# Attention with 49 of 64 block products: the row sums move from VectorE to accumulating transfers issued by GpSimd, and the scores are computed four slots earlier

## The chip, the cores and the metric

The kernel runs on one core of a Trainium2 chip. The core has TensorE (PE; its weight loads are listed as PEld), VectorE (DVE), ScalarE (ACT), GpSimd (POOL) and SyncE (SP), each with its own in-order queue, and 16 DMA engines that the queues share. SyncE issues nearly all transfers of this kernel. The metric is the device time of one execution in microseconds. Before the change the median of three runs is 3673.21 us (3672.21 to 3676.82).

## The reference, cut to what matters

Two layers are applied to x of shape (2, 512, 64, 64) in float32. The first is a deformable convolution, which the change does not touch. The second is attention over the 4096 pixels of each image:

```python
px = transpose(group_norm(x))                  # (2, 4096, 512)
q, k, v = tanh(px @ Wq.T), tanh(px @ Wk.T), px @ Wv.T
attn = softmax(einsum('bip,bjp,p->bij', q, k, align_w), axis=2)
content = (px + attn @ v) @ Wfc.T + bfc
x = x + relu(batch_norm(content))
```

So every query needs 4096 exponentials of scores, their sum (the softmax's denominator) and their product with the values. The residual px enters the same product.

## The kernel before, in words

All of the attention is in the part of the kernel that begins at L1242. The values are multiplied by Wfc ahead of time, so that one product gives the content.

**Chunks, blocks and slots.** An image is worked on in four chunks of 1024 queries, so there are eight chunks in all. The queries of a chunk are in two halves (`qh`), the keys in groups `g` of 512 (NG = 8 groups), and each group in two halves. A score tile `e0`, `e1`, `e2` or `e3` of one group holds the exponentials of one half of the keys against one half of the queries: `e0` and `e2` belong to the first query half, `e1` and `e3` to the second. Each tile has 128 partitions of 1024 numbers, 512 KB. The product with the values is a two-level scheme that needs seven products where a plain one has eight, used twice over: 7 x 7 = 49 block products in place of 64. It needs sums and differences of blocks, and these are VectorE's work. A chunk takes 7 products `p` of 9 steps each (eight groups, and a ninth for the residual), so 63 slots (SLOTS); `ORDER` (L1378) says which tile each product uses. In a slot TensorE does seven block matmuls (L1478), each recorded twice, with weights `v` that SyncE loads three slots ahead (`fetch`, L1570; four buffers).

**The order of the work.** It is written out by hand. `Attention.slot` (L1592) issues the work of one slot in program order, and each engine keeps to it. `EVENTS` (L1541) says in which slot a score tile is made; negative slots belong to the end of the chunk before, which overlaps with the start of the next one from slot 44 on. `produce` (L1389) makes a tile: two score matmuls into the one PSUM buffer `pS` and an exponential on ScalarE. `settle` (L1417) follows one slot later on VectorE. It adds a first-half tile to the running total, and replaces the second block of each tile by the difference of its two blocks (`transform`, L1385). For `e1` it also calls `second_row` (L1410), which turns `e0` into `e1 - e0` and `e1` into `e1 + e3` and adds the latter to the second half's total. `inner_sums` (L1454) makes `tt`, three more block sums, for the slot LEAD = 4 ahead; there are five buffers of `tt`.

**The row sums.** `add_total` (L1403) keeps one total per query half, `tot`. The first tile is copied, and each later one is added by VectorE. `total` (L1426) adds the two blocks of 512 numbers of the total on VectorE, in slots 4 and 21. One slot later `spread_total` (L1432) multiplies by a matrix of ones on TensorE, so that the sum over the partitions stands in all of them. TensorE waits there for `total`, and what follows on TensorE waits behind it. `scale_residual` (L1446) then multiplies the residual by the sum, and in slots 7 and 25 the reciprocal is taken. The sum for the ninth step of a product cannot be made before that. For this reason `sums` for slots 8 and 26 comes late, in slots 6 and 24.

**Buffers and start.** Score tiles, totals, residuals and products `ct` share one ring of 36 pieces (`w1ring`, L1245). At the start of each image the values are computed first (`values`, L1622). The tiles with negative slots of its first chunk are made between them (`early_scores`, L1674), and those left over in one go at the end. In that stretch GpSimd has some additions of its own (`sum_pixels`, L1303).

Of the kernel before, what the change touches and what calls it, by code (L numbers as in the profile page):

```python
# [10 lines left out]
F32 = mybir.dt.float32  # L11
I32 = mybir.dt.int32
AF = mybir.ActivationFunctionType
ALU = mybir.AluOpType
# [4 lines left out]
P = 128  # L19
# [508 lines left out]
NG = S // P // 4  # L528
# [6 lines left out]
def kernel(ctx: ExitStack, tc: tile.TileContext, t_in: dict, out: bass.AP):  # L535
# [7 lines left out]
    nc.vector.tensor_reduce(al[:, 1:2], al[:, 0:1], AX.X, ALU.max, apply_absolute_value=True)  # L543
    nc.vector.memset(al[:, 0:1], 1.0 / SCORE_MAX)
    window_path(tc, t_in, out, far, sums)


# [27 lines left out]
def window_path(ctx: ExitStack, tc: tile.TileContext, t_in: dict, out: bass.AP, far: bass.AP, sums: bass.AP):  # L575
    nc = tc.nc
# [66 lines left out]
    with ExitStack() as l0:  # L643
# [517 lines left out]
        with tc.manual_schedule():  # L1161
# [60 lines left out]
            for i in range(NSEQ):  # L1222
# [6 lines left out]
                w, m, g = Chain(weights, i + 1), Chain(sample, i), Chain(features, i + 3)  # L1229
# [12 lines left out]
    with ExitStack() as l1, tc.manual_schedule():  # L1242
        HC = C // 2
        HQ = CH // 2
        ring = l1.enter_context(tc.tile_pool(name="w1ring", bufs=36, reuse_waits="tile"))  # L1245
        bnp = l1.enter_context(tc.tile_pool(name="w1bnp", bufs=1))
        bst = bnp.tile([P, KB, NB * NCH, 6], F32, name="bst")
        bfc = load("L1_conv_bfc", [P, KB], None, bnp)
# [3 lines left out]
        def piece(name, shape=(P, 2, CH)):  # L1252
            return ring.tile(list(shape), F32, tag="r", name=name)
# [15 lines left out]
        with ExitStack() as inner:  # L1269
            wk = inner.enter_context(tc.tile_pool(name="w1work", bufs=1))  # L1270
# [94 lines left out]
            def load_queries(n, k):  # L1365
                q = wk.tile([P, 2, CH], F32, name="q")
                for h in range(2):
                    nc.sync.dma_start(q[h * DQ : (h + 1) * DQ], q_d[n][k])
                return q
# [12 lines left out]
            def blocks(t):  # L1382
                return t.rearrange("p a (s q) -> p (a s) q", s=2)

            def transform(t):  # L1385
                x = blocks(t)
                nc.vector.tensor_sub(x[:, 1], x[:, 1], x[:, 0])
# [14 lines left out]

            def add_total(c, qh, t):  # L1403
                if qh in c.tot:
                    nc.vector.tensor_add(c.tot[qh], c.tot[qh], t)  # L1405
                else:
                    c.tot[qh] = piece("tot")
                    nc.vector.tensor_copy(c.tot[qh], t)

            def second_row(c, g):  # L1410
                t0, t1 = c.e["e0", g], c.e["e1", g]
                nc.vector.tensor_sub(t0, t1, t0)  # L1412
                nc.vector.tensor_add(t1, t1, c.e["e3", g])  # L1413
                if g < NG:
                    add_total(c, 1, t1)

            def settle(c, key, g):  # L1417

                e = c.e[key, g]
                if key in ("e0", "e2"):  # L1420
                    add_total(c, 0, e)
                transform(e)
                if key == "e1":
                    second_row(c, g)

            def total(c, qh):  # L1426
                t = c.tot[qh]
                nc.vector.tensor_add(t[:, 1, :], t[:, 1, :], t[:, 0, :])
                if qh:
                    nc.vector.tensor_add(t[:, 1, HQ:], t[:, 1, HQ:], t[:, 0, :HQ])  # L1430

            def spread_total(c, qh):  # L1432
                p = pair_bank("pr")[:, 0, :]
                nc.tensor.matmul(p, ones, c.tot.pop(qh)[:, 1, :], start=True, stop=True)
                nc.scalar.copy(rin[:, qh, :], p)

            def load_residual(c, qh):
                x = load_chunk(c.n, 2 * c.k + qh, nc.sync, "xq")
                for h in range(2):
                    c.e[f"e{2 * h + qh}", NG] = x[h]  # L1440

            def norm_residual(c, qh):
                for h in range(2):
                    normalize(c.e[f"e{2 * h + qh}", NG], 2 * h, *norms[c.n])

            def scale_residual(c, qh):  # L1446
                for h in range(2):
                    t = c.e[f"e{2 * h + qh}", NG]
                    nc.vector.tensor_mul(t, t, rin[:, qh, :].unsqueeze(1).to_broadcast([P, 2, CH]))
                    transform(t)  # L1450
                if qh:
                    second_row(c, NG)
# [14 lines left out]
            def products(c, p, g, v, t):  # L1467
                if g == 0:
                    c.acc = bank("accx"), bank("accy")
                ax, ay = c.acc  # L1470
                x = blocks(c.e[ORDER[p][0], g])
                for out, blk, op, first, final in (
                    (ax[:, 0], 0, x[:, 0], True, False), (ax[:, 1], 2, x[:, 2], False, True),
                    (ax[:, 2], 4, t[:, 0], True, True),
                    (ay[:, 0], 3, t[:, 2], True, False), (ay[:, 1], 1, x[:, 1], False, True),
                    (ay[:, 2], 5, x[:, 3], True, False), (ay[:, 3], 6, t[:, 1], False, True),
                ):
                    nc.tensor.matmul(out, v[:, blk, :], op, start=(first and g == 0), stop=(final and g == NG))  # L1478

            def first_copy(c):  # L1480
                ax, ay = c.acc
                u = wk.tile([P, HQ], F32, name="u", bufs=2)
                nc.scalar.copy(u, ax[:, 0])  # L1483
                return u

# [53 lines left out]
                    yield from finish(c, t, 1, 0)  # L1539

            EVENTS = {}  # L1541
            for g, l in enumerate((-14, -13, -11, -10, -9, -7, -6, -5)):
                EVENTS.setdefault(l, []).append(("e0", g))
            for g in range(NG):
                EVENTS.setdefault(g - 4, []).append(("e2", g))
                EVENTS.setdefault(5 + g, []).append(("e3", g))
                EVENTS.setdefault(13 + g, []).append(("e1", g))

            class Attention:

# [5 lines left out]
                def before(self, l, c):  # L1556

                    for done in self.open:
                        settle(*done)
                    self.open = []  # L1560
                    for key, g in EVENTS.get(l, ()):
                        produce(c, key, g)
                        self.open.append((c, key, g))
# [10 lines left out]
                def at(self, l, c, s):  # L1574

                    if l in (-7, 8):
                        load_residual(c, int(l > 0))
                    if l in (-3, 11):
                        norm_residual(c, int(l > 0))
                    if l in (5, 22):  # L1580
                        spread_total(c, int(l > 5))
                        scale_residual(c, int(l > 5))
                    if l in (7, 25):
                        nc.vector.reciprocal(rin[:, int(l > 7), :], rin[:, int(l > 7), :])
                    if l in (6, 24):
                        self.sums(s + 2)
                    if 30 <= l < 31 + NG:
                        nc.vector.tensor_add(c.e["e3", l - 30], c.e["e0", l - 30], c.e["e3", l - 30])
                    if 40 <= l < 41 + NG:
                        nc.vector.tensor_sub(c.e["e2", l - 40], c.e["e2", l - 40], c.e["e3", l - 40])  # L1590

                def slot(self, s):  # L1592
                    k, l = divmod(s, SLOTS)
                    c = self.chunks[k]
                    nxt = self.chunks[k + 1] if k + 1 < NCH // 2 else None
                    self.fetch(s + 3)
                    if l % (NG + 1) == 0 and self.ends:
                        next(self.ends[-1], None)
                    self.before(l, c)
                    if nxt and l >= 44:  # L1600
                        if l == 44:
                            nxt.q = load_queries(self.n, k + 1)
                        self.before(l - SLOTS, nxt)
                        self.at(l - SLOTS, nxt, s)
                    self.at(l, c, s)
                    if l + LEAD not in (8, 26):
                        self.sums(s + LEAD)
                    if l in (4, 21):
                        total(c, int(l > 4))
                    p, g = divmod(l, NG + 1)  # L1610
                    products(c, p, g, self.v.pop(s), self.t.pop(s))
                    for e in self.ends[:-1] if g == 0 else self.ends:
                        next(e, None)
                    if g == NG:
                        self.ends = self.ends[-1:] + [collect(c, p, first_copy(c), c.acc)]
# [50 lines left out]
            for n in range(NB):  # L1666
# [1 line left out]
                first = at.chunks[0]  # L1668
                pending = []
                early_events = deque(  # L1670
                    (l, key, g) for l in range(-16, 0) for key, g in EVENTS.get(l, ())
                )

                def early_scores():  # L1674
# [76 lines left out]
                for done in at.open:  # L1751
                    settle(*done)
# [5 lines left out]
                for s in range(NCH // 2 * SLOTS):  # L1758
                    at.slot(s)
                    l = s - (NCH // 2 - 1) * SLOTS  # L1760
# [88 lines left out]
```

## Time and profile before

| | |
|---|---|
| median of three runs | 3673.21 us |
| the profiled execution | 3674.86 us |
| its span | 3673.1 us |
| busy: PE, PEld, DVE, ACT, POOL | 3239.0, 2261.1, 2969.6, 1362.9, 272.5 us |
| mean granted TensorE clock | 0.949 |
| DMA | 537.67 MB, 146 GB/s over the span |
| additions to `tot` at L1405 | 176, 1221 ns each, 214.9 us |
| exponentials at L1400 | 256, 1023 ns each |

Busy time counts an engine's instructions, and a wait shows as idle time before an instruction, with the instruction or transfer that released it. The attention lies between about 1300 and 3590 us of the span. The spreads of the second query half, which mark the chunks, start at 1543.5, 1791.1, 2039.4 and 2286.5 us for the first image and at 2701.1, 2948.4, 3196.7 and 3445.4 us for the second.

### The profile page before, as it was taken

To read this page: it belongs to the slowest core of one execution; us is meant where nothing else is said; L and a number is where in the kernel's file an instruction comes from. 1 tells how busy PE (TensorE), PEld (TensorE's weight loads), DVE (VectorE), ACT (ScalarE), POOL (GpSimd) and SP (SyncE) were. 2 spreads that over 40 slices of the span, in tenths; PEclk is the share of its full clock that TensorE was granted. 3 is DMA by queue.
4 is the path that set the end of the run, shared out by engine and by line. 5 is a ranking of instruction groups with operands and counts; after the bars stand their busy time and mean duration, and the time that the engine had idled before them with its cause. 6 is when DMAs were issued, how large, how long until landed. Compare 5 with 4: busy or idle time off the path is not lost.

```text
span 3673.1 us, 37956 instructions
## 1 busy us (share of the span) xinstructions
PE 3239.0 (88%) x14147; PEld 2261.1 (62%) x14147; DVE 2969.6 (81%) x4107; ACT 1362.9 (37%) x1802; POOL 272.5 (7%) x186
## 2 busy tenths in 40 slices
PE   5789999999998867899899898998889989899890
PEld 2355555555555645686676776876577676686670
DVE  8899999999995577877887878778787787877864
ACT  2577778778775312203112022022202202203105
POOL 1121121121120110000000000011000000000000
PEclk9889999999999978999999999999899999999995
DMA  6334334334232454344353443555434344344379
GB/s 211 97 116 139 120 100 127 109 108 131 94 105 102 163 198 160 117 147 151 116 160 123 135 151 108 185 175 202 156 121 154 123 142 139 113 151 146 113 299 349
DMA packets 201634, 537.67 MB, mean 146 GB/s; under 512 B 25024, under 2 KB 26816, under 8 KB 200416
## 3 DMA queue, kind: packets, MB, share of 16 engines
q1 hardware_dynamic: 193920, 514.18, 41.9%
q10 hardware_dynamic: 7488, 20.97, 1.7%
q8 instruction: 113, 1.85, 0.2%
q14 instruction: 81, 0.66, 0.1%
q0 software_dynamic: 32, 0.00, 0.0%
HBM read 410.15 MB, written 124.91 MB: 146 GB/s over the span
## 4 chain that ended last, share of the span: by engine, by line
PE 63%; DVE 27%; DMA 4%; ACT 3%; issue 1%; POOL 1%; SPq 0%; ACTq 0%; DVEq 0%; POOLq 0%
PE accy L1478 20%; PE accx L1478 16%; DVE conv L820 9%; PE py L1004 6%; PE pS L1396 5%; PE pq L789 5%; PE pa L984 5%; DVE tot L1405 2%; DVE e L1412 2%; DVE e L1413 2%; PE pvy L1633 2%; PE pk L1700 1%; DVE tt L1458 1%; DVE vform L1332 1%; PE pvx L1633 1%
## 5 line engine op out<-in xcount | busy, mean ns | idle before, releaser
L1478 PE MATMUL accy<-tt,v 128*128 128x256 f32 x2016 | 602.2, 380 | 0.0
L1400 ACT ACTIVATE e<-pS 128x1024 f32<-128x1024 f32 x256 | 261.8, 1023 | 895.0 <-PE pS L1396 785.6
L1478 PE MATMUL accx<-e,v 128*128 128x256 f32 x1792 | 489.1, 396 | 25.8 <-DMA v<-wv 15.3
L1478 PEld LDWEIGHTS accx<-e,v 128*128 128x128 f32 x1792 | 329.5, 193 | 226.4 <-issue 153.1
L1478 PE MATMUL accy<-e,v 128*128 128x256 f32 x1792 | 461.7, 380 | 0.0
L820 DVE SCALAR_TENSOR_TENSOR conv<-xn,L_conv_dw_w_sb,conv 128x504 f32<-128x504 f32 (+1 forms) x512 | 409.4, 808 | 36.6 <-ACT conv L814 22.7
L1478 PEld LDWEIGHTS accy<-tt,v 128*128 128x128 f32 x2016 | 385.0, 191 | 53.0
L1478 PEld LDWEIGHTS accy<-e,v 128*128 128x128 f32 x1792 | 342.5, 191 | 47.3
L1396 PE MATMUL pS<-q,keys 64*128 64x512 f32 x1024 | 294.7, 653 | 35.1 <-ACT e L1400 25.5
L1458 DVE TENSOR_TENSOR tt<-tt,e 128x512 f32<-128x512 f32 x448 | 310.0, 692 | 15.3
L1478 PE MATMUL accx<-tt,v 128*128 128x256 f32 x1008 | 302.8, 382 | 0.0
L1457 DVE TENSOR_TENSOR tt<-e 128x256 f32<-128x256 f32 x448 | 187.6, 419 | 140.9 <-PE accy L1478 139.8
L984 PEld LDWEIGHTS pa<-bt,patch 96*128 96x128 f32 x2048 | 249.6, 196 | 57.1 <-issue 35.1
L984 PE MATMUL pa<-bt,patch 96*128 96x128 f32 x2048 | 253.1, 280 | 7.0 <-ACT bt L970 5.6
L970 ACT COPY bt<-pb 96x1024 f32<-96x1024 f32 x124 | 234.8, 2009 | 57.8 <-PE pb L965 53.9
L1483 ACT COPY u<-accx 128x256 f32<-128x256 f32 x56 | 20.9, 373 | 619.5 <-PE accx L1478 619.5
L789 PE MATMUL pq<-in_w,xn 128*128 128x512 f32 x512 | 239.3, 611 | 7.1 <-DVE o L882 5.0
L1004 PE MATMUL py<-dT,L_conv_out_w_sb 128*128 128x512 f32 x512 | 237.6, 609 | 4.7 <-ACT dT L995 4.7
L1405 DVE TENSOR_TENSOR tot<-tot,e 128x1024 f32<-128x1024 f32 x176 | 214.9, 1221 | 29.1 <-ACT e L1400 27.1
L1478 PEld LDWEIGHTS accx<-tt,v 128*128 128x128 f32 x1008 | 193.8, 192 | 27.1
L877 PE MATMUL po<-om_w_pg,feat 128*128 128x432 f32 x512 | 202.9, 540 | 3.0 <-ACT feat L860 3.0
L995 ACT COPY dT<-pa 32x256 f32<-32x256 f32 x496 | 179.6, 362 | 66.3 <-PE pa L984 57.0
(215 smaller groups left out, 4316.2 us busy)
## 6 DMA issues: line engine op xcount, KB each, us to landing
v<-wv SPq DMA_DIRECT2D x448, 448.0 KB
wv<-vform SPq DMA_DIRECT2D x112, 448.0 KB
patch<-xt SPq DMA_DIRECT2D x256, 192.0 KB
v<-ww SPq DMA_DIRECT2D x56, 448.0 KB
xt<-xj SPq DMA_DIRECT2D x128, 128.0 KB
res<-in_x SPq DMA_DIRECT2D x64, 256.0 KB
wx<-res SPq DMA_DIRECT2D x64, 256.0 KB
xq<-wx SPq DMA_DIRECT2D x32, 512.0 KB
```

The costliest lines, as they stand in the source:

```text
L789: nc.tensor.matmul(pq, xn[:, kb, 1 + 2 * t : 3 + 2 * t, :].rearrange("p r c -> p (r c)"), in_w[:, kb, :], start=(kb == 0), stop=(kb == KB ...
L820: nc.vector.scalar_tensor_tensor(dst, src, wt, dst, ALU.mult, ALU.add)
L877: nc.tensor.matmul(po[:, : 3 * GP], f[:, kb, t * P : (t + 1) * P], om_w[:, kb].rearrange("p a k g -> p (a k g)"), start=(kb == 0), stop=(k ...
L970: copy(bt[:SN].rearrange("s g q d -> s d (g q)")[:, d0 : d0 + 4, :], pb[:SN])
L984: nc.tensor.matmul(pa[:, p], xp[:SN, p, cb * P : (cb + 1) * P], bt[:SN, 4 * cb : 4 * cb + 4, PX * s + p, :], start=True, stop=True,)
L1004: nc.tensor.matmul(py, out_w[:, kb, cb * P : (cb + 1) * P], dT[:, kb, :], start=(kb == 0), stop=(kb == KB - 1))
L1396: nc.tensor.matmul(p[:, a, :], keys[r, i, (2 * u + h) * P : (2 * u + h + 1) * P], c.q[r, qh, :], start=True, stop=True)
L1400: nc.scalar.activation(e.rearrange("p a q -> p (a q)"), p.rearrange("p a q -> p (a q)"), AF.Exp)
L1405: nc.vector.tensor_add(c.tot[qh], c.tot[qh], t)
L1457: nc.vector.tensor_sub(t[:, 0], x[:, 1], x[:, 3])
L1458: nc.vector.tensor_add(t[:, 1:3], t[:, 0].unsqueeze(1).to_broadcast([P, 2, HQ]), x[:, 0:3:2])
L1478: nc.tensor.matmul(out, v[:, blk, :], op, start=(first and g == 0), stop=(final and g == NG))
```

## The change

`add_total` no longer adds on VectorE. GpSimd issues a transfer from the tile to the total, within SBUF, that adds each number to what stands there. Since the next transfer reads and writes the same total, it has to wait for the one before. `settle` now calls `transform` ahead of `add_total`, so the totals of the first half are those of transformed tiles, and `total` makes the extra addition for both halves. Scores are made earlier: `e0` in slots -18 to -11, `e2` in -9 to -2, `e3` in 0 to 7, `e1` in 9 to 18 with two slots left out. The overlap with the next chunk begins at slot 43. For the second half `total` moves from slot 21 to 22 and the spread from 22 to 23. The ring gets 38 pieces, and the small tile `u` one buffer in place of two.

```diff
-        ring = l1.enter_context(tc.tile_pool(name="w1ring", bufs=36, reuse_waits="tile"))
+        ring = l1.enter_context(tc.tile_pool(name="w1ring", bufs=38, reuse_waits="tile"))
...
                 if qh in c.tot:
-                    nc.vector.tensor_add(c.tot[qh], c.tot[qh], t)
+                    nc.gpsimd.dma_start(c.tot[qh], t, accum_op=ALU.add)
                 else:
                     c.tot[qh] = piece("tot")
                     nc.vector.tensor_copy(c.tot[qh], t)
...
                 e = c.e[key, g]
+                transform(e)
                 if key in ("e0", "e2"):
                     add_total(c, 0, e)
-                transform(e)
                 if key == "e1":
                     second_row(c, g)
 
             def total(c, qh):
                 t = c.tot[qh]
                 nc.vector.tensor_add(t[:, 1, :], t[:, 1, :], t[:, 0, :])
-                if qh:
-                    nc.vector.tensor_add(t[:, 1, HQ:], t[:, 1, HQ:], t[:, 0, :HQ])
+                nc.vector.tensor_add(t[:, 1, HQ:], t[:, 1, HQ:], t[:, 0, :HQ])
...
-                u = wk.tile([P, HQ], F32, name="u", bufs=2)
+                u = wk.tile([P, HQ], F32, name="u")
...
             EVENTS = {}
-            for g, l in enumerate((-14, -13, -11, -10, -9, -7, -6, -5)):
-                EVENTS.setdefault(l, []).append(("e0", g))
-            for g in range(NG):
-                EVENTS.setdefault(g - 4, []).append(("e2", g))
-                EVENTS.setdefault(5 + g, []).append(("e3", g))
-                EVENTS.setdefault(13 + g, []).append(("e1", g))
+            for g, l in enumerate((9, 10, 12, 13, 14, 16, 17, 18)):
+                EVENTS.setdefault(g - 18, []).append(("e0", g))
+                EVENTS.setdefault(g - 9, []).append(("e2", g))
+                EVENTS.setdefault(g, []).append(("e3", g))
+                EVENTS.setdefault(l, []).append(("e1", g))
...
-                    if l in (5, 22):
+                    if l in (5, 23):
                         spread_total(c, int(l > 5))
                         scale_residual(c, int(l > 5))
...
-                    if nxt and l >= 44:
-                        if l == 44:
+                    if nxt and l >= 43:
+                        if l == 43:
                             nxt.q = load_queries(self.n, k + 1)
...
-                    if l in (4, 21):
+                    if l in (4, 22):
                         total(c, int(l > 4))
...
-                    (l, key, g) for l in range(-16, 0) for key, g in EVENTS.get(l, ())
+                    (l, key, g) for l in range(-18, 0) for key, g in EVENTS.get(l, ())
```

## The prediction

> **What bounds the kernel now.** I read the page's chain and groups first. TensorE carries 63% of the chain that ended last and VectorE 27%, so the question is where the VectorE share lies. The list of waits, between 1300 and 3550 us, answers it (engine, line, releaser: total us, times, longest):
>
> ```profile
> PE pr L1434 <- DVE tot L1430: 82.5, 8, 10.3
> PE pS L1396 <- ACT e L1400: 25.5, 28, 1.2
> ```
>
> Eight times, once per chunk, TensorE waits 10.3 us for the row sums of the second query half. TensorE's timeline around one of them (start, duration, instruction, idle before it):
>
> ```profile
> 1780.17 0.59 PE L1478 MATMUL accy<-tt,v 128*128 128x256 f32 x2
> 1791.08 2.05 PE L1434 MATMUL pr<-tot,ones_k 128*128 128x512 f32 x2 [10.32 <-DVE tot L1430]
> 1792.92 1.91 PE L1478 MATMUL accx<-e,v 128*128 128x256 f32 x4
> ```
>
> The spread takes 2.05 us here against 1.12 us for the other one of the chunk, and the next matmuls 1.91 against 1.13: after the pause TensorE runs slow for a while. The slot after it takes 3.8 us in one chunk and 4.6 in the next, against 3.02. The pause so costs 10.3 + 0.9 + 0.8 to 1.6, about 12.4 us. One whole chunk, from spread to spread (columns: PE, PEld, DVE, ACT, POOL busy, granted clock, DMA share, GB/s):
>
> ```profile
> 1545.57:1793.13 247.56, 234.66 (x1015) 176.33 (x1015) 199.27 (x279) 47.26 (x57) 0.00 (x0) 0.98 0.43 136
> ```
>
> TensorE idles 12.9 us: 10.3 in this pause, 1.1 before the other spread, twice 0.73 before a score. Why VectorE is late shows in its timeline, one slot with a score of the second half:
>
> ```profile
> 1778.30 0.42 DVE L1387 TENSOR_TENSOR e<-e 128x256 f32<-128x256 f32 x1
> 1778.76 1.23 DVE L1412 TENSOR_TENSOR e<-e 128x1024 f32<-128x1024 f32 x1
> 1780.02 1.23 DVE L1413 TENSOR_TENSOR e<-e 128x1024 f32<-128x1024 f32 x1
> 1781.28 1.23 DVE L1405 TENSOR_TENSOR tot<-tot,e 128x1024 f32<-128x1024 f32 x1
> 1782.42 0.42 DVE L1457 TENSOR_TENSOR tt<-e 128x256 f32<-128x256 f32 x1
> 1782.87 0.69 DVE L1458 TENSOR_TENSOR tt<-tt,e 128x512 f32<-128x512 f32 x1
> ```
>
> That is 5.2 us, against 4.28 us of TensorE for a slot with a score (1746.12 to 1750.40 in its timeline). Over eight such slots VectorE falls behind by some 8 us, which with other VectorE work makes the pause. L1405 is the part that the change takes away.
>
> **What the skill says.** "DMA: Bandwidth & Descriptors", section "SWDGE vs HWDGE vs iDMA": an accumulate in a transfer is for GpSimd's software path only. In that page's "Rules for kernel authors", an accumulate reads its destination and writes it later, so the next one has to wait for the earlier semaphore: the additions into one total form a chain, one whole latency each. The same page, "Anatomy of one DMA", gives a software-path transfer about 2.0 us plus bytes at 436 GB/s, that is 3.2 us for 512 KB. The trace has slower plain ones. "Collectives: The Full Stack", "The bandwidth ceiling", says that an adding transfer reads two sources and so has half a copy's rate. No run here shows an accumulate yet. What the trace has is a plain transfer of the same 512 KB in the chain of waits (start, us), and one small transfer from GpSimd's queue:
>
> ```profile
> 2578.32 4.26 DMA xq<-wx
> ...
> L542 POOL DMA_DIRECT2D al_f<-in_L_conv_align_w x1: 656/656/656, 1.2 to 1.2; - x1
> ...
> DMA to landing us min/median/max: 6.9/6.9/6.9
> ```
>
> The last is 0.2 KB, issued at 1.2 us while the first megabytes were being loaded.
>
> **The change, part by part.** Call T the time of one link: wait seen, descriptors, move, semaphore.
> *Removed from VectorE:* 176 additions of 1.22 us (215 us busy), hidden everywhere but in the second-half slots, where 5.2 us becomes 3.95, under TensorE's 4.28. The new spacing also leaves slots 11 and 15 without a score. From slot 9 to 22 TensorE has 8 x 4.28 + 6 x 3.02 = 52.4 us. VectorE has 8 x 2.9 settling + 0.7 copy + 13 x 1.1 inner sums + two collections of 2.5 + 3.7 for finishing + 1.1 for the total = 48 us. It keeps up, with little to spare; I allow 1 us per chunk.
> *Added to VectorE:* one addition of 0.42 us to the first total, 8 times: it lies in the 5.9 us that VectorE idles there.
> *The pause* goes if the sums are in time: 8 x 12.4 = 99 us.
> *Scores earlier, 38 pieces, one u.* Counting births and last reads of the pieces, the peak per slot rises from 37 to 39 while the ring grows from 36 to 38, so one late score still waits for a piece. It is now the last (slot 18), with no score behind it before the spread at 23. The two waits of 0.73 us per chunk go: 8 x 1.46 = 12 us. One u is enough, since it is filled once in nine slots and read in the next. The queries are asked for two slots (6 us) before their first use instead of five; their two transfers take 2.1 us to issue on the SyncE queue behind one values load, so they should land some 5 us after the slot begins. Cover gone, this would cost a microsecond per chunk.
> *The later spread:* from it to the inner sum of slot 26 stand 0.65 us for the copy, 5.8 us of residual work and two sums of 1.1: 8.7 us, where three slots give 9.1. It fits barely.
> *Each image's start:* sixteen scores instead of twelve precede the first product, each 2.3 us of score and exponential in series (3.2 on the slow clock), but four slots get 1.26 us shorter and about eight additions leave the VectorE stretch that ends it (L1405 stands between the L1338 lines until 2588). I take 4 us gained per image, 8 in all.
> *What is behind the new waits:* GpSimd's queue holds only these transfers in the slots, so an early wait hurts no one. But the total (slots 4, 22) waits on VectorE for the last link, behind it stand all inner sums, and TensorE's spread comes a slot later; TensorE has four slots of sums in hand, so the spread is what is late.
>
> Free time for the chains: *first total*, fifteen links from slot -16 to the spread in slot 5: 19 slots of 4.28 + 2 of 3.02 + 2.2 (score and its exponential already in front of the spread) - 1.6 for the work at both ends = 88 us, 5.87 per link. *Second total*, seven links from slot 11 to 23: 43.8 us - 2.9 settling - 1 late - 1.1 total = 38.8, 5.55 per link. *First chunk of each image:* the scores come bunched; counted from 2558 in the old trace, 13 links have until some 2618 us: 4.6 each.
>
> *T:* lower end 4.26 + 0.34 (656 ns of issue against SyncE's 320) = 4.6, the second read wholly hidden. With the second read not hidden at the rate of the last window (362 GB/s at 0.94 share: 1.36 us) it is 6.0. Upper end: al_f's 6.9 plus 1.36, 8.2. In the slots a values load of 448 KB stands in the queue every 3 to 4 us, but the mean share is only 0.43, and the 4.26 was measured at 0.72 (2580 to 2600 us). I take 5.6.
>
> Sum, on the profiled execution's 3674.9 us (span 3673.1 and 1.8 around it): - 99 - 12 - 8 + 8 = 3564 with all chains in time. At T = 5.6 add 2 x 13 x 1.0 = 26 at the image starts, 7 x 0.05 x 8 = 3 at the second totals and 4 for the clock: 3597. The median of the runs is 1.7 us below that execution, hence 3596, 2.1% faster.
>
> **Rivals.** *The chain becomes the bound (slower).* Place: the spreads in slots 5 and 23. Each 0.1 us of T over the limits costs 2.6 us at the starts, 6 x 1.5 = 9 at the first totals and 8 x 0.7 = 5.6 at the second ones, and 2.1 us of slow clock per pause. At T = 6.0: 36 + 12 + 25 + 25 = 98, which is 3662. Break-even is T = 6.05; at 6.8: 57 + 84 + 70 + 34, which is 3809; at 7.0, 3843. For it: 6.9 us of a tiny transfer, two reads, and the software path's preparation. Against: that transfer stood behind the first loads. *VectorE stays late.* If reordering leaves it 5 us behind at slot 22, 40 us of the pause stay: 3637. For it: 48 of 52 us is tight and collections come in lumps; TensorE's four slots of sums speak against. *The transfers disturb the values loads.* They add 22 x 512 KB per chunk, 47 GB/s read twice, to 136 GB/s; the share would go from 0.43 to about 0.7. Values are asked for three slots, 9 us, ahead, and even the 6.4 us that one took at the image start fits: cost nil, but it lengthens T.
>
> **How the numbers follow.** Chain in time or nearly: 0.43, 3560 to 3625, my forecast. VectorE late or T near 6: 0.10, up to 3665. Break-even: 0.04. Chain late: 0.43, of which 0.25 up to 3850 and the rest above. So faster 0.53, same (within 0.2%, about what a measurement of this kernel can tell) 0.04, slower 0.43, and a range of 3555 to 3850.
>
> **What would show it.** Right: the wait for L1430 shrinks from 10.3 us to under 3, slots of 4.28 us throughout, 176 transfers on GpSimd's queue with about 5.6 us from one to the next where they are bunched, and a chunk of some 235 us. Wrong: a spread in slot 5 or 23 waiting for a total that waits for a transfer, links of over 6 us, and the DMA share well over 0.7.

## The result, and the profile after

The changed kernel takes 3716.23 us (median of three runs, 3715.81 to 3722.25) against 3673.21 us: the ratio is 1.012, with a 95% interval of 1.0097 to 1.0143. It is slower by 1.2%, where 2.1% less had been forecast. The span of the profiled execution went from 3673.1 to 3714.0 us.

The list of waits of the changed kernel, from 1300 to 3600 us (engine, line, releaser: total us, times, longest):

```profile
DVE tot L1428 <- DMA tot<-e: 164.3, 16, 21.8
...
PE pr L1433 <- DVE tot L1429: 120.5, 16, 16.0
...
PE pS L1396 <- ACT e L1400: 22.7, 20, 1.2
```

Before, TensorE waited at one spread per chunk, 82.5 us in all, for a VectorE that was behind with its additions. Now it waits at both, 120.5 us, for a total that itself waits for a transfer. The 20 waits left before scores are those of the image starts; the sixteen of 0.73 us in the slots are gone. TensorE's timeline at the two spreads of the second chunk, and VectorE's at the first of them:

```profile
1735.64 2.04 PE L1433 MATMUL pr<-tot,ones_k 128*128 128x512 f32 x2 [13.31 <-DVE tot L1429]
1809.73 2.04 PE L1433 MATMUL pr<-tot,ones_k 128*128 128x512 f32 x2 [3.38 <-DVE tot L1429]
```

```profile
1713.82 1.28 DVE L1494 BATCH_NORM_STATS2 bst<-ct 128x6 f32<-128x512 f32 x2
1715.01 0.41 DVE L1387 TENSOR_TENSOR e<-e 128x256 f32<-128x256 f32 x1
1734.38 0.69 DVE L1428 TENSOR_TENSOR tot<-tot 128x512 f32<-128x512 f32 x1 [18.96 <-DMA tot<-e]
```

VectorE has nothing left to do at 1715.4 and stands for 19 us until the last link of the chain has landed. The links before it, on GpSimd's timeline:

```profile
1712.87 0.86 POOL L1405 DMA_DIRECT2D tot<-e  x1 [4.86 <-DMA tot<-e]
1719.28 0.86 POOL L1405 DMA_DIRECT2D tot<-e  x1 [5.56 <-DMA tot<-e]
1725.02 0.86 POOL L1405 DMA_DIRECT2D tot<-e  x1 [4.87 <-DMA tot<-e]
1729.91 0.86 POOL L1405 DMA_DIRECT2D tot<-e  x1 [4.04 <-DMA tot<-e]
```

Each is released by the one before: 6.4, 5.7 and 4.9 us from issue to issue. The instructions on the total in the whole run (count, then duration min/median/max in ns), and their time from issue to landing:

```profile
L1405 POOL DMA_DIRECT2D tot<-e x176: 852/859/877, 1360.1 to 3479.0; - x176
...
DMA to landing us min/median/max: 4.4/5.4/10.3
```

The chunk from the second spread to the next one, columns as before:

```profile
1556.50:1811.80 255.30, 238.34 (x1016) 178.44 (x1015) 173.88 (x258) 47.37 (x57) 18.91 (x22) 0.96 0.65 178
```

VectorE is relieved as planned, from 199 to 174 us, and the DMA share rises from 0.43 to 0.65. But the chunk takes 255.3 us in place of 247.6, with TensorE idle for 17.0 us in place of 12.9 and busy for 3.7 us more, since it runs slow after two pauses instead of one.

Where the 40.9 us of span lie, by the first and the last product matmul of each image in TensorE's timeline:

| stretch | before | after | difference |
|---|---|---|---|
| start to the first product | 1436.4 | 1436.7 | +0.3 |
| products of image 0 | 977.7 | 1008.1 | +30.4 |
| from there to the products of image 1 | 180.3 | 189.7 | +9.4 |
| products of image 1 | 981.4 | 981.9 | +0.5 |
| the rest | 97.3 | 97.6 | +0.3 |

In the product stretches, 30.9 us in sum, the waits at the spreads grew by 29.0 (120.5 against 82.5 and 8 times 1.12) and the waits before scores fell by 11.7. A wait that the kernel before does not have adds 9.2 us:

```profile
PE accy L1477 <- DVE ct L1507: 9.2, 8, 2.1
```

Once per chunk, after the second spread, TensorE stands before a new product until VectorE has begun to collect the sums of the last one (`ct`), since the new accumulator takes the PSUM bank that this collection reads. Nearly all of the remaining 4.4 us is busy time of TensorE. It rises by 4.0 us although four scores per image, 1.26 us each (4.28 against 3.02 us for a slot), have moved out of these stretches. TensorE runs slow more often: 13 of the 16 spreads now take 2.04 or 2.05 us, against 8 before.

### The profile page after: what moved, and what is told of

The parts are those of the page before. It is cut to its first block, busy times and chain, and to the rows that moved or that the text cites. A ratio compares the mean times of both kernels' runs of the same rounds, so it can differ in the third digit from the quotient of the medians.

```text
span 3714.0 us, 38267 instructions
## 1 busy us (share of the span) xinstructions
PE 3251.5 (88%) x14147; PEld 2267.2 (61%) x14147; DVE 2763.9 (74%) x3939; ACT 1363.3 (37%) x1802; POOL 424.1 (11%) x362
## 5 line engine op out<-in xcount | busy, mean ns | idle before, releaser
L1405 POOL DMA_DIRECT2D tot<-e x176 | 151.3, 860 | 1751.9 <-DVE e L1387 699.6
L1396 PE MATMUL pS<-q,keys 64*128 64x512 f32 x1024 | 302.3, 668 | 32.7 <-ACT e L1400 22.7
```

What stands on the lines that cost most here:

```text
L1396: nc.tensor.matmul(p[:, a, :], keys[r, i, (2 * u + h) * P : (2 * u + h + 1) * P], c.q[r, qh, :], start=True, stop=True)
```

## The experiments

Two theories were put against each other. A: each link takes longer than its place allows, so the chain of transfers is what costs. B: the transfers are harmless, and the moved slots cost. All edits are to the changed kernel. The times are medians. The waits of TensorE at the spreads, from the one profiled run of each kernel, are summed over the eight chunks (each first spread has at least 1.12 us behind an exponential, 9.0 in sum). With transfers in the second half only and with half tiles the profiled run is the slowest of its kernel (3635.3 and 3648.6 us):

| kernel | time, us | ratio to before | at first spreads | at second spreads |
|---|---|---|---|---|
| before | 3673 | | 9.0 | 82.5 |
| changed | 3716.2 | 1.012 [1.0097, 1.0143] | 91.0 | 29.5 |
| sums on VectorE | 3612.0 | 0.983 [0.9814, 0.9847] | 9.0 | 23.6 |
| two chains in the first half | 3627.8 | 0.9873 [0.9856, 0.9889] | 9.0 | 28.2 |
| transfers in the second half only | 3619.9 | 0.9845 [0.9828, 0.9861] | 9.0 | 39.3 |
| half tiles | 3638.5 | 0.9903 [0.9886, 0.9919] | 30.7 | 26.1 |
| plain copies | 3589.3 (one run) | | 9.0 | 0.5 |
| half the values | 3639.1 (one run) | | 48.8 | 0.0 |
| sums on VectorE, forms first | 3595.5 | 0.9784 [0.9768, 0.9801] | 9.0 | 23.4 |
| ... and three transfers | 3595.9 | 0.9783 [0.9767, 0.98] | 9.0 | 26.7 |
| ... and five transfers | 3594.9 | 0.9778 [0.9765, 0.9792] | 9.0 | 20.3 |

**The additions back on VectorE, with the new slots.**

```diff
-                    nc.gpsimd.dma_start(c.tot[qh], t, accum_op=ALU.add)
+                    nc.vector.tensor_add(c.tot[qh], c.tot[qh], t)
```

> The changed kernel with its new slots, but with the additions back on VectorE (nothing left out). Theory A (the chain of accumulating transfers is what costs): the pauses at the first spread go, and the one at the second spread is VectorE's own, about 5 us (VectorE then has 48 + 7 x 1.22 = 56.5 us of work from slot 9 to 22 against TensorE's 52.4), so about 3630 us, faster than both kernels. Theory B (the moved slots cost, the transfers do not): 3700 us or more, with the changed kernel's loss still there.

Measured: 3612.0 us, 1.7% faster than before and 104 us less than the changed kernel. So the change holds two opposite parts. Everything but the transfers (scores two to six slots earlier, the second spread one slot later, the ring and `u`) wins 61 us, and the transfers lose 104. B falls. The wait at the second spread, 10.3 us before, is 2.95 us now with all additions on VectorE: this rearrangement does most of what the transfers were for. Which of its parts does it, the second row's scores spaced over ten slots or the later spread, was not measured.

**Two chains for the first half.** Tiles alternate between two totals.

```diff
-                if qh in c.tot:
-                    nc.gpsimd.dma_start(c.tot[qh], t, accum_op=ALU.add)
+                pair = c.tot.setdefault(qh, [])
+                if len(pair) < 2 - qh:
+                    pair.append(piece("tot"))
+                    nc.vector.tensor_copy(pair[-1], t)
                 else:
-                    c.tot[qh] = piece("tot")
-                    nc.vector.tensor_copy(c.tot[qh], t)
+                    nc.gpsimd.dma_start(pair[0], t, accum_op=ALU.add)
+                    pair.reverse()
...
-                t = c.tot[qh]
+                t, *more = c.tot[qh]
+                c.tot[qh] = t
+                for x in more:
+                    nc.vector.tensor_add(t, t, x)
```

> The changed kernel with two totals for the first query half, each with every other tile, added up at the end by one more VectorE addition (nothing left out); the second half keeps one chain. Theory A: the pauses at the first spread (91 us in sum) go and with them some 2 us of slow clock each, those at the second (30 us) stay: about 3716 - 91 - 16 = 3609 us. If transfers slow one another when two are under way, so that two links take as long as one after the other, the pauses stay: 3700 us. Theory B: 3716 us.

The waits at the first spreads are gone with the same number of transfers but eight, and in the same slots. So it is the order of one chain that costs, not the traffic. Single transfers become slower, with a median of 6.3 us from issue to landing against 5.4, but two run side by side. The total is 19 us above the 3609 expected. Ten of them are a later first product (1446.9 against 1436.7 us), and 6 a longer stretch between the images (196.0 against 189.7). Of the 91 us in the expectation only 82 could go, since 9.0 stand at the first spreads in every kernel; TensorE's busy time in the product stretches fell by 21 us in return, where 16 had been expected of the slow clock.

**Transfers in the second half only.**

```diff
-                    nc.gpsimd.dma_start(c.tot[qh], t, accum_op=ALU.add)
+                    if qh:
+                        nc.gpsimd.dma_start(c.tot[qh], t, accum_op=ALU.add)
+                    else:
+                        nc.vector.tensor_add(c.tot[qh], c.tot[qh], t)
```

> The changed kernel with accumulating transfers for the second query half alone; the first half's additions are back on VectorE, which has room there (nothing left out). Theory A: the first spreads no longer pause, the second ones as in the changed kernel: about 3609 us, as with two chains. Theory B: 3716 us. If VectorE's extra 1.22 us in the first half's slots now meets the second row's work: some 10 us more.

As A expects at the first spreads. The second ones vary from 2.4 to 8.2 us in the profiled run, where the transfers take 4.6 to 8.1 us from issue to landing: a chain that decides the end hands such differences on. The four runs spread too (3610.9 to 3635.3 us), while the kernel without transfers stays within about 5 us. Whether the chain is what spreads them is not shown, since only the slowest run was profiled, and with two chains in the first half, where late second totals also decide, the runs stay within 3 us.

**Each transfer in two halves.**

```diff
-                    nc.gpsimd.dma_start(c.tot[qh], t, accum_op=ALU.add)
+                    for a in range(2):
+                        nc.gpsimd.dma_start(c.tot[qh][:, a, :], t[:, a, :], accum_op=ALU.add)
```

> The changed kernel with each accumulating transfer cut into two of 256 KB for the two blocks of 512 numbers, each its own chain (nothing left out). Theory A with a link that is mostly fixed latency: no gain, the two halves take turns on GpSimd's queue, about 3716 us. Theory A with a link that is mostly data movement in turn with other transfers: the halves overlap, a pair takes about 1.6 us less than a full link, so 15 x 1.6 = 24 us less at each first total, enough to remove the pauses: about 3590 to 3620 us.

In between: 78 us less than the changed kernel, with a third of the first spreads' waits left, in the slowest of its runs. A half lands after 3.2 us at least and 4.7 in the median, against 4.4 and 5.4 for a whole one. The least falls by 1.2 us, which is what the packets of a half save: eight on each DMA engine, of 178 ns in place of 328 (medians). By this count moving the data is 2.6 us (8 x 328 ns) of the 4.4 us, and the rest stays when the size is halved. Two halves under way together can pay that rest at the same time, which fits the gain.

**Plain copies.**

```diff
-                    nc.gpsimd.dma_start(c.tot[qh], t, accum_op=ALU.add)
+                    nc.gpsimd.dma_start(c.tot[qh], t)
```

> The changed kernel with plain copies in place of the accumulating transfers, same sizes, same waits (this leaves out the additions: the total is the last tile). Measures what the second read costs in a link. If an accumulate moves at half a copy's rate, packets of 4 KB take 160 ns instead of 328 and a link is about 1.35 us shorter: mean 5.0 us, pauses nearly gone, about 3600 us. If the latency is all that counts, the mean link stays at 6.4 us and the time at 3716 us.

The instructions on the total and their landing:

```profile
L1405 POOL DMA_DIRECT2D tot<-e x176: 527/530/561, 1364.7 to 3353.6; - x176
...
DMA to landing us min/median/max: 2.8/3.5/8.1
```

From issue to landing an addition takes 1.9 us more than a copy (5.4 against 3.5), of which 0.33 us is a longer issue. In the trace a packet of 4 KB of these transfers takes 328 ns (median) with the addition and 159 ns without. Every second spread but one is reached without any wait (the one has 0.49 us), so with VectorE relieved, nothing but the links was late there. This run also measures the rest of the change with the chains in time: 3589 us, where the prediction's sum was 3564. Against the 3612.0 us with all sums on VectorE, links this short would have made VectorE's relief worth 23 us (one run). And it shows the new wait in full:

```profile
PE accy L1477 <- DVE ct L1507: 16.9, 8, 2.1
```

VectorE's timeline in it, from the residual work that the second spread releases to this collection, has no gap:

```profile
1534.28 1.23 DVE L1448 TENSOR_TENSOR xq<-xq,rin 128x1024 f32<-128x1024 f32 x1 [1.85 <-ACT rin L1434]
...
1543.06 3.35 DVE L1582 RECIPROCAL rin<-rin 128x512 f32<-128x512 f32 x1
...
1548.39 0.68 DVE L1507 TENSOR_TENSOR ct<-u,accx 128x512 f32<-128x512 f32 x1
```

In the kernel before (there L1508), with one slot more between the spread and the collection, it was VectorE that waited there:

```profile
1560.36 0.69 DVE L1508 TENSOR_TENSOR ct<-u,accx 128x512 f32<-128x512 f32 x1
1561.68 0.69 DVE L1509 TENSOR_TENSOR ct<-ct,accy 128x512 f32<-128x512 f32 x1 [0.64 <-PE accy L1478]
```

By these timelines the wait, 2.1 us per chunk, is the price of the later spread; no run varies that alone.

**Half of the values loads.**

```diff
-                        self.v[s] = load_values(self.n, *divmod(s % SLOTS, NG + 1))
+                        p, g = divmod(s % SLOTS, NG + 1)
+                        if g % 2 and s - 1 in self.v:
+                            self.v[s] = self.v[s - 1]
+                        else:
+                            self.v[s] = load_values(self.n, p, g)
```

> The changed kernel with every other values load left out (odd groups use the weights of the even group before; this changes the products). Measures what the competing transfers add to a link. If the loads in turn with the links make them 6.4 us instead of the 4.9 us of the shortest: mean link about 5.6 us, pauses at most a third, about 3630 us. If links are long by themselves: mean 6.4 us, 3716 us.

```profile
DMA to landing us min/median/max: 4.4/4.6/10.9
```

The median falls from 5.4 to 4.6 us and the fastest stays at 4.4. So a link is at its shortest 4.4 us to landing and, from the closest starts in the trace, 4.9 from issue to issue; the values loads left out here had added 0.8 us to the median. Over six first totals (those of the image starts apart) the mean from issue to issue falls from 6.53 to 5.95 us, close to the 5.87 that was free. The waits at the second spreads vanish, and half of the first ones' stay, mainly the two image starts (16.1 and 14.3 us).

**The image start.** In the first experiment the stretch between the images is 191.4 us, against 180.3 before, and the products of image 1 begin so:

```profile
2560.74 2.08 PE L1396 MATMUL pS<-q,keys 64*128 64x512 f32 x4 [1.12 <-ACT e L1400]
2571.83 2.04 PE L1477 MATMUL accx<-e,v 128*128 128x256 f32 x4 [9.01 <-DMA v<-wv]
```

The scores are done, and TensorE waits for the first values. These come from the last forms, which stand on VectorE behind the settling of the leftover scores, one every 3.2 us. The edit puts the forms first:

```diff
                     if i == 3:
+                        while pending:
+                            for _ in pending.pop(0):
+                                pass
                         while early_events:
```

> The kernel of the first experiment (new slots, additions on VectorE), with the last value forms of each image put ahead of the scores left over at the image start (nothing left out). If the later start of the second image's products comes from VectorE settling scores in order ahead of the forms whose values TensorE then waits for: the stretch between the two images' products falls from 191 to about 182 us, the first start by some 4 us, so about 3599 us. If the ten scores in series set the start by themselves: no change, 3612 us.

The stretch falls to 182.3 us, and the first image's products begin at 1434.2 in place of 1440.9. The time is 3595.5 us, 17 us less, and 2.2% under the kernel before, with no accumulating transfer at all. What is left are 23.4 us at the second spreads and 15.8 us of waits for the collection at L1507.

**A few transfers on top.** Groups 1 to 3 (then 1 to 5) of the second half by transfer; the group after them is added together with the next one. The edit for three, cut to the second row (`add_total` gets a third argument that chooses the transfer); for five, 5 and 4 become 7 and 6, and `g < 4` becomes `g < 6`:

```diff
-                if g < NG:
-                    add_total(c, 1, t1)
+                if g == 5:
+                    add_total(c, 1, c.e["e1", 4])
+                if g < NG and g != 4:
+                    add_total(c, 1, t1, 0 < g < 4)
```

> The kernel with the forms first, and in addition three of the second half's seven additions (groups 1 to 3) as accumulating transfers, which are finished before VectorE adds groups 4 to 7 to the same total from slot 17 on (nothing left out). If the 2.95 us pause at the second spread is VectorE's backlog of additions, and three early transfers have time enough: the pause goes and with it about 1.4 us of slow clock, 8 x 4.3 = 35 us less than the kernel with the forms first, about 3565 us. If the transfers are late even there, VectorE waits for the third one in slot 17: 3600 us or more.

> As the kernel with three transfers, but groups 1 to 5 of the second half are added by transfers and only 6 and 7 by VectorE, in slot 19 (nothing left out). If the three early transfers gave nothing because VectorE idled early and its backlog is made by the last additions (slots 17 to 19): two more of those go, 2.44 us, the pause falls from 3.34 to about 0.9 us, and with the slow clock 8 x 3.5 = 28 us go: about 3568 us. If the fifth link is not done when VectorE adds groups 6 and 7: pauses of 3 us and more, 3595 us.

Neither wins: 3595.9 and 3594.9 us. The links are in time now, and the waits at the second spread are VectorE's, 3.34 and 2.54 us each against 2.93. In its timeline with three transfers it idles early (1.17 us for a `tt` buffer and 0.97 for an exponential around 1498) and gives the relief back. From 1499.9 on it has no gap until the total at 1525.4. With five transfers it idles too before the last stretch, which still holds a collection of four sums for `ct`, the settling of two tiles, both additions (2.47 us) and the finishing of `ct`. By these timelines the wait is made by that lump in the last slots, and additions taken away ahead of it do not shorten it. Starting the total before the finishing of `ct` was not tried.

## Why the prediction was wrong

**What bounds the kernel** was read rightly. The 10.3 us came from VectorE's lateness in the second row's slots, and where VectorE is relieved and the links are in time (plain copies), the second spreads do not wait. But the rearrangement alone takes 7.4 of the 10.3 us away, so the transfers had less to win than the prediction gave them.

**The step that failed is T**, the time of one link, taken as 5.6 us. In six first totals (all but those of the image starts) the links average 6.53 us (6.1 to 6.8 by chunk), in the second totals 6.20, and in the last thirteen links of the image starts 6.6 and 6.4. The terms, for those six first totals:

| term of a link, us | prediction | measured |
|---|---|---|
| plain transfer from GpSimd, issue to landing | 4.26 + 0.34 | 3.97 (plain copies, mean) |
| what the addition adds | 1.0 of 1.36 | 1.91 (mean 5.88 to landing) |
| from landing to the next issue | nothing | 0.53 |
| the rest, when a tile was not ready | nothing | 0.12 |
| link | 5.6 | 6.53 |

The addition and the step from landing to the next issue were 1.4 us too small together. The half rate that the prediction took over from collectives does show in the packets, 328 against 159 ns, which is 1.35 us for eight of them; the mistake was to let a part of it be hidden. That the plain transfer was taken 0.6 us too long made up for some of this, by luck. Part of the means is traffic: with half of the values loads the links average 5.95 us, where the prediction argued from the DMA share of 0.43 that the loads add nothing.

The 4.26 us were also misread. In the trace of before, VectorE's addition at the end of that piece of the chain follows the instruction before it without a gap, so it did not wait for the transfer. ScalarE did:

```profile
2578.32 1.01 SPq L1297 DMA_DIRECT2D xq<-wx  x2
```

```profile
2582.23 0.42 DVE L1387 TENSOR_TENSOR e<-e 128x256 f32<-128x256 f32 x1
2582.58 1.22 DVE L1405 TENSOR_TENSOR tot<-tot,e 128x1024 f32<-128x1024 f32 x1
```

```profile
2583.74 2.93 ACT L1290 ACTIVATE xq<-xq,gn_bi,gn_sc 128x512 f32<-128x512 f32 x4 [1.99 <-DMA xq<-wx]
```

From issue to its reader this transfer took 5.4 us. With 5.4 in place of 4.26 the prediction's own sum gives a T of 6.7 and "slower". That would have been right with another wrong term, since plain copies within SBUF turned out faster than this load.

**The free times held.** With 6.73 us per link in the second chunk the first total needs 15 x 6.73 = 101 us where 88 were allowed, 13 us late; the wait is 13.3, of which 1.1 stands there in every kernel. The second needs 7 x 6.12 = 42.8 where 38.8 were allowed, 4.0 late; it is 3.4. The rival that forecast "slower" named this mechanism, place and point of decision (6.05 us). Its rates give 6 x 15 x (6.53 - 5.87) = 59 us at the first totals (57.2 measured beyond the 1.1 each) and 8 x 7 x (6.20 - 5.55) = 36 at the second (29.5 measured). The image starts were overrated: the rates give 2 x 13 x (6.5 - 4.6) = 49 us there, and 25 were measured beyond the 1.1 each. So was the slow clock, taken as 2.1 us per pause: with the same matmuls in the product stretches TensorE is busy for 22.9 us longer than with plain copies, 1.4 us for each of 16 spreads. The two cases stood at 0.43 each, and the forecast went to the one with T 0.45 us below break-even, which the first totals missed by 0.5.

**The sum without late chains failed too, as a smaller term.** With plain copies the kernel takes 25 us more than the 3564. Of these, 15.5 lie at the image starts: the forecast gained 8 us there, and the kernel with copies begins 3.9 us later and takes 3.6 more between the images (the changed kernel 0.3 and 9.4). The prediction counted the scores' series and VectorE's relief, but not that VectorE settles in order, so that each extra score held up the forms behind it; the run with the forms first shows this for the kernel with sums on VectorE. Another 17 us are the waits at L1507. The prediction checked what stands between the later spread and the sum for slot 26, but not the collection behind it. Against that, the 8 us allowed for a late VectorE at the second spread were not needed. The small terms left have not been traced. (The last step of the forecast, 3597 less 1.7, gives 3595 and not 3596.)

**Right, and seen in the profile:** the two 0.73 us waits per chunk went; one `u` and the later query load cost nothing that shows; in the attention no engine waits for GpSimd itself; the slow clock followed most pauses.

## What to carry to other kernels

A chain of dependent transfers is paid link by link: before work is moved into one, count its links, multiply by the whole time from issue to issue under the traffic of that stage, and hold this against the time until the first reader; near the threshold, split the chain or leave it. A step of a chain of waits counts as a transfer's time only where the reader's timeline shows that it waited. Where a change has several parts, measure each alone: here the rearrangement was the gain and the transfers, its apparent point, the loss. An engine that works in order also hands a delay to everything issued behind it, so work that feeds the next stage goes ahead of work that waits.

## What the runs showed of the hardware

- An accumulating transfer of 512 KB within SBUF takes 4.4 us at least from issue to landing and 5.4 in the median of this kernel; a plain copy of the same form from the same queue takes 2.8 and 3.5. GpSimd is occupied for 0.86 us by the first and 0.53 by the second, both within these times. From landing to the issue that waits for it pass 0.53 us.
- A 4 KB packet takes 328 ns with the addition and 159 ns without, a 2 KB packet 178 ns with it (medians).
- Cut into two halves under way together, a transfer's half takes 3.2 us at least and 4.7 in the median from issue to landing. Two chains side by side raise the median of whole transfers to 6.3 us, and the first totals are still in time where one chain is late.
- Leaving out half of the 448 KB values loads beside the chain lowers its median landing from 5.4 to 4.6 us and leaves the least at 4.4.
